# The projection behind a scan: stored expert terms by plain loads, sums on GpSimd, weights turned in the scan's first rounds, roots of two sequences at once

## The chip, the cores and the metric

The kernel runs on one core of a Trainium2 chip. The core has a matmul engine (PE; its weight loads are listed as PEld), a vector engine (DVE), an activation engine (ACT), GpSimd (POOL) and SyncE (SP), which here only issues transfers. Each engine works through its own instructions in order, and the DMA engines work beside them. The metric is the device time of one execution in microseconds (us). All times below are us unless ns is written.

## The reference, cut to what matters

The input `x` is 8 sequences of 1,024 tokens with 256 channels, in 32-bit floats. Two layers follow one another, each of them x plus a sequence mixer plus a mixture of experts, both taken from the same layernorm:

```python
xn = layernorm(x)
# mixer of layer 0: per channel d a state of 16 numbers
h = einsum('dnm,bdm->bdn', A, h) + Bm * x_t
y_t = einsum('dn,bdn->bd', Cm, h) + Dm * x_t
y = gelu(layernorm(y, ln_w, ln_b)) @ W_out.T + b_out
x = x + (xn + y) + experts0(xn)      # 8 experts, 2 of them per token, and a shared one
xn = layernorm(x)
# mixer of layer 1: the softmax runs over an axis of length 1, so every weight is 1
values = sum of (xn @ w_v.T) over the sequence
x = x + values @ w_o.T + experts1(xn)   # 8 experts of 2,048 places, 2 per token
```

The first layer's experts have 128 hidden channels, the second's 1,024. In the second layer a token's gate is its two largest softmax scores divided by their sum.

## The kernel before, in words

Tokens lie on 128 partitions, a tile is 128 tokens: a sequence has 8 tiles (`TPB`), all of them 64 (`NT`). The whole `y`, 64 tiles of 256 channels, stays on the chip. The kernel has five stages.

*Layernorm and first routing (up to about 185).* The normalised `xn` goes into an SBUF tile with rows of `XW` = 264 numbers, of which 256 are used. The shared expert and x are written to an array in DRAM, `base`.

*Finds (about 185 to 288).* The routing has given each pair of a token and an expert a place among 71 blocks (142 columns `NCOL`) of 128 rows. `find` (L694 to L719, 32 calls: 2 choices times 16 groups of 4 tiles) makes one-hot tables on DVE: `hl` says which row (L702), the plane `hh[:, :, 0]` which column (L705); the plane `hh[:, :, 1]` is that times the pair's number plus one, taken from a table `tags` (L709); then plane 0 is multiplied by the token's number in its tile (L712). Four matmuls (L716) sum both into `acc`, and `found` (L721) reads the lists from it.

*Scan (about 288 to 893).* The 256 channels are handled in 8 batches of 32. A batch makes its filters by doubling (`krylov`, levels 1 to 64: matmul L309, copies L316 on DVE and L317 on ACT), carries states from tile to tile (`chunk`: matmul L383, addition L390) and computes outputs (matmul L363, L414) with `xn` as the stationary operand. The blocks of the experts (`block`) are woven in: gather `xb`, matmuls L258 and L269, result `yo` (L767), which an indirect write puts into the DRAM array `yr` (L770), two rows for a token, one for each choice. The loop at the end of the scan deals out finds, blocks, krylov levels and batch steps in one order; finds come during the first batch.

*Projection (893 to 1166).* First `W_out`, `w_o` and the value rows of `w_qkv` are loaded on ACT's queue, turned by PE (L862) and multiplied (L881). Then for every sequence b:

- `start(b)`: a load of `base` into `hb` on SP's queue (L933), two transfers on POOL's queue that add the two rows of `yr` to it (L938), and the moments of `y` (L164, L165, root L166, reciprocal L167);
- `turn(b)`: `off` (L180), 8 normalises on ACT (L182), and matmuls with a flip matrix that turn the tiles, with the gelu (L908) on the way out of PSUM;
- `project(b)`: matmuls with `woutT` (L956), and `y` = PSUM + `hb` on DVE (L963);
- `finish(b)`: moments of the new `y`, `xs` = normalised (L182), its write to `xd`, transposes (L898, copied L904 with sums over tokens), the router's matmuls (L918) and the copy to `logit` (L978);
- `attend(b)`: the token sums spread by POOL (L985), a matmul (L988), `at` (L992), a plain write of `y` to the output (L994) and a transfer on POOL's queue that adds `at` to it (L995);
- `route`, after every second sequence for 16 tiles and after sequences 6 and 7 for 8 tiles each: maximum, exponential (L1007), sum, reciprocal, product, the two best experts, ranks, tables (`hl` L1060, `hh` L1065, L1069, ACT L1073, PE L1075). The first call also runs `no_expert` (L1081).

The order is `start(b+1)`, `project(b)`, `turn(b+1)`, `finish(b)`, `route`, `attend(b)` (L1106 to L1120). A scheduler places the instructions of each engine; the waits between engines follow from the tiles and their buffers.

*Second layer's experts (1166 to 2132).* Gather (L1197), two matmuls (L1213, L1239), and an indirect addition to the output (L1251).

Of the kernel before, what the change touches and what calls it, by code (L numbers as in the profile page):

```python
# [18 lines left out]
P = 128  # L19
# [5 lines left out]
def kernel(  # L25
# [131 lines left out]
    def moments(pool, src, n, mv=None, rstd=None):  # L157

        st = pool.tile([P, n, 6], F32, name="st")
        if mv is None:  # L160
            mv = pool.tile([P, n, 2], F32, name="mv")
            rstd = pool.tile([P, n], F32, name="rstd")
        for i in range(n):
            nc.vector.bn_stats(st[:, i, :], src[:, i, :])  # L164
            nc.vector.bn_aggr(mv[:, i, :], st[:, i, :])  # L165
        nc.scalar.activation(rstd, mv[:, :, 1], AF.Sqrt, bias=epst)  # L166
        nc.vector.reciprocal(rstd, rstd)  # L167
        return mv, rstd

    def normalize(dst, src, mv, rstd, n):  # L170
        for i in range(n):
            nc.vector.tensor_scalar(
                dst[:, i, :], src[:, i, :], mv[:, i, 0:1], rstd[:, i : i + 1],
                ALU.subtract, ALU.mult,
            )

    def normalize_act(dst, src, mv, rstd, n, pool):

        off = pool.tile([P, n], F32, name="off")
        nc.vector.scalar_tensor_tensor(off, mv[:, :, 0], -1.0, rstd, ALU.mult, ALU.mult)  # L180
        for i in range(n):
            nc.scalar.activation(  # L182
                dst[:, i, :], src[:, i, :], AF.Identity,
                bias=off[:, i : i + 1], scale=rstd[:, i : i + 1],
            )
# [23 lines left out]
    with tc.tile_pool(name="xpool", bufs=1) as xpool, tc.tile_pool(name="mo", bufs=2) as mo, tc.tile_pool(  # L209
# [8 lines left out]
        xn = xpool.tile([P, NT, XW], F32, name="xn")  # L218
# [13 lines left out]

        tags = xpool.tile([P, 2, NT], BF16, name="tags")
        nc.gpsimd.iota(tags, pattern=[[1, 2], [2, NT]], base=1, channel_multiplier=0,
                       allow_small_or_imprecise_dtypes=True)

# [43 lines left out]
        def krylov(bt):  # L280
# [23 lines left out]
            def level(k):  # L304
                for g in groups:
                    t = m[g]
                    pk = ps_k.tile([P, 2, 2 * P], F32, name="pk")
                    for j in range(2):
                        nc.tensor.matmul(  # L309
                            pk[:, j, : P + k],  # L310
                            lhsT=t[:, 1 - j, P:],
                            rhs=t[:, j, P - k :],
                            start=True,
                            stop=True,
                        )
                    nc.vector.tensor_copy(t[:, :, P - 2 * k : P - k], pk[:, :, :k])  # L316
                    nc.scalar.copy(t[:, :, P:], pk[:, :, k : k + P])  # L317
# [3 lines left out]
        def rest(bt, toep):  # L321
# [4 lines left out]
            def responses():  # L326
# [26 lines left out]
                nc.vector.memset(made["h"][:, :, :, 0], 0.0)  # L353
# [21 lines left out]
            def chunk(c):  # L375
# [5 lines left out]
                ph = ps_m.tile([P, 512], F32, name="pm")  # L381
                for j, g in enumerate(groups):
                    nc.tensor.matmul(  # L383
                        ph[:, j * NB : (j + 1) * NB],
                        lhsT=m[g][:, 1, P:],
                        rhs=h_t[:, j, :, c],
                        start=True,
                        stop=True,
                    )
                nc.vector.tensor_tensor(  # L390
                    h_t[:, :, :, c + 1],
                    ph[:, : GB * NB].rearrange("p (g b) -> p g b", g=GB),
                    s_t[:, :, :, c],
                    ALU.add,
# [294 lines left out]
        with tc.tile_pool(name="eb", bufs=3) as eb_, tc.tile_pool(name="toep", bufs=2) as toep:  # L689
# [4 lines left out]
            def find(k, i):  # L694
# [11 lines left out]
                    hh[:, :, 0, :], bc(names, 1, [P, 4, NCOL]),  # L706
                    bc(high0[:, k, four], 2, [P, 4, NCOL]), ALU.is_equal,
                )
                nc.vector.tensor_tensor(  # L709
                    hh[:, :, 1, :], hh[:, :, 0, :], bc(tags[:, k, four], 2, [P, 4, NCOL]), ALU.mult  # L710
                )
                nc.vector.tensor_scalar(  # L712
                    hh[:, :, 0, :], hh[:, :, 0, :], tokid[:, 0:1], None, ALU.mult
                )
# [63 lines left out]


# [4 lines left out]
            ] + [found]  # L784
            for bt in range(NBT):
# [9 lines left out]
                for s, step in enumerate(steps):  # L795
                    step()
                    if s % 2 == 0 and s // 2 < len(ahead):
                        ahead[s // 2]()
                    for f in part(s):
# [3 lines left out]
    with tc.tile_pool(name="wmoe", bufs=1) as wmoe, tc.tile_pool(name="tr", bufs=2) as tr, tc.tile_pool(  # L803
        name="xr", bufs=3
    ) as xr, tc.tile_pool(name="rt", bufs=2) as rt, tc.tile_pool(
        name="r1", bufs=1
    ) as r1, tc.tile_pool(name="hot", bufs=2) as hotp, tc.tile_pool(
        name="ps_t", bufs=3, space=PSUM
    ) as ps_t, tc.tile_pool(name="ps_d", bufs=2, space=PSUM) as ps_d, tc.tile_pool(
        name="ps_c", bufs=1, space=PSUM  # L810
    ) as ps_c, tc.tile_pool(name="ps_i", bufs=1, space=PSUM) as ps_i:
# [4 lines left out]
        vals = r1.tile([P, 2, NT], F32, name="vals")  # L816


        QALL = NTOK // P
        place = r1.tile([P, P], BF16, name="place")  # L820
        nc.gpsimd.iota(place, pattern=[[1, P]], base=0, channel_multiplier=0,
                       allow_small_or_imprecise_dtypes=True)
        column = r1.tile([P, 2, E, QPE], F32, name="column")
        for j in range(2):
            nc.gpsimd.iota(column[:, j], pattern=[[QALL, E], [1, QPE]], base=j * (QALL - QPE),
                           channel_multiplier=0, allow_small_or_imprecise_dtypes=True)
        column = column.rearrange("p k e q -> p k (e q)")
        offset = r1.tile([P, 2, E], F32, name="offset")
        nc.gpsimd.iota(offset[:, 0, :], pattern=[[NTOK, E]], base=0, channel_multiplier=0,
                       allow_small_or_imprecise_dtypes=True)  # L830
        nc.gpsimd.iota(offset[:, 1, :], pattern=[[-NTOK, E]], base=1 - NTOK, channel_multiplier=0,
                       allow_small_or_imprecise_dtypes=True)
        sign = r1.tile([P, 2, 2 * TPB], F32, name="sign")
        nc.gpsimd.memset(sign[:, 0, :], 1.0)
        nc.gpsimd.memset(sign[:, 1, :], -1.0)
        go_on = {}
        for n in (TPB, 2 * TPB):
            go_on[n] = r1.tile([P, 2, E, n + 1], F32, name=f"go_on{n}")
            nc.gpsimd.memset(go_on[n], 1.0)
            nc.gpsimd.memset(go_on[n][:, :, :, 0], 0.0)  # L840
        logit = r1.tile([P, 2 * TPB, E], F32, name="logit")
        rowno = r1.tile([P, 2, QPE], F32, name="rowno")
        nc.gpsimd.iota(rowno[:, 0, :], pattern=[[P, QPE]], base=0, channel_multiplier=1,
                       allow_small_or_imprecise_dtypes=True)
        nc.gpsimd.iota(rowno[:, 1, :], pattern=[[-P, QPE]], base=CAP - 1, channel_multiplier=-1,
                       allow_small_or_imprecise_dtypes=True)
        few = r1.tile([P, E], F32, name="few")
        pi = [ps_i.tile([P, 2, P], F32, name=f"pi{j}") for j in range(2)]
        lnw_c = wmoe.tile([P, DC], F32, name="lnw_c")
        nc.scalar.dma_start(lnw_c, ln_w.rearrange("(c p) -> p c", p=P))  # L850
        lnb_c = wmoe.tile([P, DC], F32, name="lnb_c")
        nc.scalar.dma_start(lnb_c, ln_b.rearrange("(c p) -> p c", p=P))

# [440 lines left out]
```

## Time and profile before

| what | us |
| --- | --- |
| three runs, median (lowest to highest) | 2141.95 (2139.48 to 2146.34) |
| the profiled execution | 2139.14 |
| its span in the trace | 2137.4 |
| mean granted PE clock | 0.929 |
| last indirect write of `yr` lands | 895.1 |
| first `xs` normalise (sequence 0) | 939.24 |
| last one (sequence 7) | 1129.41 |
| first matmul of the second layer's experts | 1177.03 |

The times in the trace count from the start of the span. 1.74 us of the profiled execution lie outside the span. Busy time says how long an engine worked in a stretch; the chain of waits says what each instruction that came late had waited for. In a row of groups, the columns are line, engine, operation, output and inputs with their sizes, how many, then busy time, mean ns of one, and the engine's idle time before them with what ended it.

### The profile page before, as it was taken

How to read it: one execution, taken by the hardware profiler on the slowest of the kernel's cores; microseconds unless marked ns; L12 is line 12 of the kernel's file. 1: busy time of each engine (PE TensorE's matmuls, PEld its weight loads, DVE VectorE, ACT ScalarE, POOL GpSimd, SP SyncE). 2: the span in 40 equal slices, each digit the busy share in tenths (PEclk: the TensorE clock that was granted, in tenths of full speed). 3: DMA queues.
4: the chain of work that ended last, by engine and by line, in shares of the span. 5: the costliest groups of instructions: out<-in, count | busy, mean ns of one | idle time of the engine just before them, and what ended most of it. 6: DMA issues, size and time to landing. Idle time of an engine off the chain costs nothing.

```text
span 2137.4 us, 24028 instructions
## 1 busy us (share of the span) xinstructions
PE 1896.7 (89%) x8619; PEld 1409.7 (66%) x8619; DVE 710.9 (33%) x2125; ACT 662.0 (31%) x1450; POOL 811.2 (38%) x818
## 2 busy tenths in 40 slices
PE   6997879888888989577884899999999999999997
PEld 6885558767767776466773466666666666666665
DVE  5878964333334434336665010001010001010000
ACT  4641103222222221167773222222222222222221
POOL 0000021545555556421111644445445455444422
PEclk9998769899999999788886899999999999999999
DMA  9999033444454545599977223232322232232211
GB/s 301 208 197 159 0 99 87 139 140 133 125 154 130 157 136 158 160 218 235 204 157 174 59 38 75 38 79 37 74 38 55 58 60 55 35 77 35 38 20 20
DMA packets 233542, 233.15 MB, mean 109 GB/s; under 512 B 54536, under 2 KB 208976, under 8 KB 233296
## 3 DMA queue, kind: packets, MB, share of 16 engines
q0 software_dynamic: 75584, 104.98, 26.1%
q1 hardware_dynamic: 155152, 124.25, 21.3%
q10 hardware_dynamic: 2688, 2.40, 0.4%
q8 instruction: 68, 1.11, 0.2%
q14 instruction: 50, 0.41, 0.1%
HBM read 136.87 MB, written 97.85 MB: 110 GB/s over the span
## 4 chain that ended last, share of the span: by engine, by line
PE 46%; DVE 4%; ACT 3%; DMA 2%; issue 2%; POOL 0%; ACTq 0%; POOLq 0%; DVEq 0%; SPq 0%
PE phe L1213 21%; PE poe L1239 20%; PE pd L956 2%; PE pd L918 1%; DMA hb<-yr 1%; ACT xs L182 1%; DVE xTe L1208 1%; PE pt L900 1%; DVE st L164 1%; DMA out_dram<-yo,invi 1%; PE pi L1075 1%; PE pc L988 0%; PE pt L898 0%; DVE y L963 0%; DMA hb<-base 0%
## 5 line engine op out<-in xcount | busy, mean ns | idle before, releaser
L1213 PE MATMUL phe<-xTe,w1t 128*128 128x512 f32 x1024 | 450.7, 598 | 16.3 <-DVE xTe L1208 16.3
L1239 PE MATMUL poe<-w2t,hT 128*128 128x256 f32 x2048 | 450.5, 380 | 6.9 <-issue 6.6
L1239 PEld LDWEIGHTS poe<-w2t,hT 128*128 128x128 f32 x2048 | 389.9, 190 | 75.8 <-issue 24.4
L1251 POOL DMA_INDIRECT out_dram<-yo,invi x128 | 204.1, 1595 | 429.9 <-ACT yo L1250 234.5
L1213 PEld LDWEIGHTS phe<-xTe,w1t 128*128 128x128 f32 x1024 | 192.8, 191 | 255.5 <-issue 221.5
L1220 ACT ACTIVATE hT<-phe,b1T 128x512 f32<-128x512 f32 x256 | 175.9, 687 | 306.5 <-PE phe L1213 242.1
L1246 DVE TENSOR_TENSOR yo<-poe,b2t 128x512 f32<-128x512 f32 x64 | 44.3, 692 | 515.5 <-PE poe L1239 487.2
L1250 ACT ACTIVATE yo<-yo,gr 128x256 f32<-128x256 f32 x128 | 58.0, 500 | 422.3 <-DVE yo L1246 422.3
L309 PE MATMUL pk<-kr 128*128 128x129 f32 (+6 forms) x896 | 154.9, 312 | 18.2 <-ACT kr L317 16.8
L309 PEld LDWEIGHTS pk<-kr 128*128 128x128 f32 x896 | 138.4, 207 | 49.1 <-ACT kr L317 22.9
L770 POOL DMA_INDIRECT yr<-yo,goes x142 | 143.1, 1007 | 63.5 <-DVE yo L767 35.0
L258 PE MATMUL pgu<-xT,wb 128*128 128x256 f32 x568 | 148.4, 405 | 14.3 <-ACT xT L247 9.0
L756 POOL DMA_INDIRECT xb<-xnd,choice x142 | 142.1, 1001 | 45.8 <-issue 37.5
L1197 POOL DMA_INDIRECT xg<-xd,invi x128 | 124.3, 971 | 49.2 <-issue 32.0
L317 ACT COPY kr<-pk 128x256 f32<-128x256 f32 x224 | 81.1, 374 | 194.5 <-DVE kr L316 157.6
L1225 POOL DMA_INDIRECT gr<-gd,invi x128 | 124.0, 969 | 45.2 <-issue 36.3
L258 PEld LDWEIGHTS pgu<-xT,wb 128*128 128x128 f32 x568 | 113.6, 206 | 33.8 <-ACT xT L247 10.3
L751 POOL COPY wb<-wrow 1x1 int32<-1x1 int32 x71 | 14.4, 203 | 303.4 <-issue 195.1
L1231 DVE TENSOR_TENSOR gr<-gr,taken 128x4 f32<-128x4 f32 x32 | 5.3, 167 | 343.7 <-DMA gr<-gd,invi 343.7
L269 PE MATMUL pd<-wb,hh 128*128 128x256 f32 x284 | 83.2, 420 | 21.9 <-DVE hh L266 21.3
L263 ACT ACTIVATE sg<-pgu 128x256 f32<-128x256 f32 x87 | 33.4, 384 | 202.8 <-PE pgu L258 149.7
L269 PEld LDWEIGHTS pd<-wb,hh 128*128 128x128 f32 x284 | 55.0, 209 | 46.0 <-DVE hh L266 26.9
(304 smaller groups left out, 2504.1 us busy)
## 6 DMA issues: line engine op xcount, KB each, us to landing
wb<-wpk SPq DMA_DIRECT2D x71, 384.0 KB
xnd<-xn SPq DMA_DIRECT2D x8, 2048.0 KB
hk<-kscr SPq DMA_DIRECT2D x32, 512.0 KB
hb<-yr POOLq DMA_DIRECT2D x16, 1024.0 KB
y<-in_L_attn_x_dram SPq DMA_DIRECT2D x8, 1024.0 KB
base<-bout_t SPq DMA_DIRECT2D x8, 1024.0 KB
base<-y POOLq DMA_DIRECT2D x8, 1024.0 KB
hb<-base SPq DMA_DIRECT2D x8, 1024.0 KB
```

Of the source, the lines that this page charges most:

```text
L258: nc.tensor.matmul(pgu[:, j, :], lhsT=ww[:, c, :], rhs=xT[:, c, :], start=(c == 0), stop=(c == DC - 1),)
L269: nc.tensor.matmul(pd[:, q, :], lhsT=hh[:, q * P : (q + 1) * P], rhs=down, start=True, stop=True)
L309: nc.tensor.matmul(pk[:, j, : P + k], lhsT=t[:, 1 - j, P:], rhs=t[:, j, P - k :], start=True, stop=True,)
L317: nc.scalar.copy(t[:, :, P:], pk[:, :, k : k + P])
L756: nc.gpsimd.indirect_dma_start(out=xb[:, q, : D + 1], out_offset=None, in_=xnd[:, :], in_offset=bass.IndirectOffsetOnAxis(ap=choice[:, 2 * ...
L770: nc.gpsimd.indirect_dma_start(out=next(yr_own)[:, :], out_offset=bass.IndirectOffsetOnAxis(ap=goes[:, 2 * n + q : 2 * n + q + 1], axis=0) ...
L1197: nc.gpsimd.indirect_dma_start(out=xg[:, q, :], out_offset=None, in_=xd[:, :], in_offset=bass.IndirectOffsetOnAxis(ap=invi[:, q0 + q : q0 ...
L1213: nc.tensor.matmul(ph, lhsT=w1t[:, c, h * P : (h + 1) * P], rhs=xT[:, c], start=(c == 0), stop=(c == DC - 1),)
L1220: nc.scalar.activation(hT[:, h], ph, AF.Relu, bias=b1T[:, e * HC + h : e * HC + h + 1])
L1225: nc.gpsimd.indirect_dma_start(out=gr[:, q, :], out_offset=None, in_=gd[:, :], in_offset=bass.IndirectOffsetOnAxis(ap=invi[:, q0 + q : q0 ...
L1239: nc.tensor.matmul(po[:, r, :], lhsT=hT[:, h, q + r, :], rhs=w2t[:, h, :], start=(h == 0), stop=(h == HC - 1),)
L1251: nc.gpsimd.indirect_dma_start(out=of[:, :], out_offset=bass.IndirectOffsetOnAxis(ap=invi[:, q0 + r : q0 + r + 1], axis=0), in_=yo[:, r, : ...
```

## The change

It touches the scan's small parts and most of the projection.

1. `xn`'s rows are 256 numbers long, not 264.
2. `find`: the table `tags` and its multiply on DVE are gone; four multiplies by constants on ACT make plane 1.
3. `krylov`, last level: the first of a group's two matmuls and the ACT copy leave out what nothing reads.
4. `chunk`: each matmul takes the whole state tile of a group (64 columns) and the addition picks the column; the whole tile is set to zero before, not one column in eight.
5. The turning of the weights moves into the list of finds (before the 5th and the 9th call); it borrows the buffers of `wb` and `yo` and loads on ACT's queue. `lnw_c`, `lnb_c` and `wg_t` are loaded on ACT's queue at the kernel's start.
6. `first_moments`, at the last step of the last batch: moments of sequences 0 and 1, one root for both, and the normalise of sequence 0.
7. `load(b)` takes the place of `start(b)`: `base` and the two rows of `yr` by plain loads on SP's queue, added on POOL (for sequence 0 on DVE). `attend` adds `at` to `y` on POOL and writes the output once.
8. One root serves the new `y` of sequence b and the scan's `y` of sequence b + 2 (`measure_two`, `scales`).
9. `route` keeps the exponentials as they are, without sum, reciprocal and product. Sequences 6 and 7 are both routed after the last `finish`, which goes in halves. A small exponential (`ready`) is written before them.
10. The first two experts' `w1` are loaded during sequences 4 and 5. Pools are rearranged: `hb`, `xs` and `yk` have 2 buffers each (`hb` and `xs` had 3), `xT` one (2 before).

```diff
-        xn = xpool.tile([P, NT, XW], F32, name="xn")
+        xn = xpool.tile([P, NT, D], F32, name="xn")
...
                     for j in range(2):
+                        n = k if last and j == 0 else P + k
                         nc.tensor.matmul(
-                            pk[:, j, : P + k],
+                            pk[:, j, :n],
                             lhsT=t[:, 1 - j, P:],
-                            rhs=t[:, j, P - k :],
+                            rhs=t[:, j, P - k : P - k + n],
...
+                    if last:
+                        nc.scalar.copy(t[:, 1, P:], pk[:, 1, k : k + P])
+                    else:
+                        nc.scalar.copy(t[:, :, P:], pk[:, :, k : k + P])
...
-                nc.vector.memset(made["h"][:, :, :, 0], 0.0)
+                nc.vector.memset(made["h"], 0.0)
...
                 for j, g in enumerate(groups):
                     nc.tensor.matmul(
-                        ph[:, j * NB : (j + 1) * NB],
-                        lhsT=m[g][:, 1, P:],
-                        rhs=h_t[:, j, :, c],
-                        start=True,
-                        stop=True,
+                        ph[:, j], lhsT=m[g][:, 1, P:], rhs=h_t[:, j], start=True, stop=True
                     )
...
-                nc.vector.tensor_tensor(
-                    hh[:, :, 1, :], hh[:, :, 0, :], bc(tags[:, k, four], 2, [P, 4, NCOL]), ALU.mult
-                )
                 nc.vector.tensor_scalar(
-                    hh[:, :, 0, :], hh[:, :, 0, :], tokid[:, 0:1], None, ALU.mult
+                    hh[:, :, 0, :], hh[:, :, 1, :], tokid[:, 0:1], None, ALU.mult
                 )
+                for t in range(4):
+                    nc.scalar.mul(hh[:, t, 1, :], hh[:, t, 1, :], float(1 + 2 * (i + t) + k))
...
+            def turn_weights(src, dst):
+                wt = wide("wb")
+                nc.scalar.dma_start(wt, src.rearrange("(r p) d -> p r d", p=P))
+                pm = ps_m.tile([P, 512], F32, name="pm")
+                for c in range(DC):
+                    for r in range(DC):
+                        nc.tensor.transpose(
+                            pm[:, (c * DC + r) * P : (c * DC + r + 1) * P],
+                            wt[:, r, c * P : (c + 1) * P], ident,
+                        )
+                nc.scalar.copy(dst.rearrange("p c d -> p (c d)"), pm)
...
+            def first_moments():
+                for b in range(2):
+                    moments(mo, first_mv[:, b], y[:, b * TPB : (b + 1) * TPB, :], TPB)
+                scales(first_mv, first_rstd, first_off)
+                ys = y[:, :TPB, :]
+                normalize_act(ys, ys, first_rstd[:, 0], first_off[:, 0], TPB)
...
+            finds[4:4] = [lambda: turn_weights(W_out, woutT)]
+            finds[9:9] = [value_weights]
...
+                    if bt == NBT - 1 and s == len(steps) - 1:
+                        first_moments()
...
-            for j in range(2):
-                nc.gpsimd.dma_start(hb, both[j], accum_op=ALU.add)
-            hold[b] = hb, moments(rt, y[:, b * TPB : (b + 1) * TPB, :], TPB)
+            for t in range(0, TPB, 4):
+                some = slice(t, t + 4)
+                yk = xr.tile([P, 4, 2, D], F32, name="yk")
+                nc.sync.dma_start(yk, both[:, some])
+                for j in range(2):
+                    (nc.gpsimd if b else nc.vector).tensor_tensor(
+                        hb[:, some, :], hb[:, some, :], yk[:, :, j, :], ALU.add
+                    )
+            hold[b] = hb
...
+        def measure_two(b):
+            n = 2 if b + 2 < NB else 1
+            mv = rt.tile([P, n, TPB, 2], F32, name="mv")
+            if n == 2:
+                moments(rt, mv[:, 1], y[:, (b + 2) * TPB : (b + 3) * TPB, :], TPB)
...
-            mine = of[b * S : (b + 1) * S, :].rearrange("(i p) d -> p i d", p=P)
-            nc.sync.dma_start(mine, y[:, b * TPB : (b + 1) * TPB, :])
-            nc.gpsimd.dma_start(mine, bc(at, 1, [P, TPB, D]), accum_op=ALU.add)
+            ys = y[:, b * TPB : (b + 1) * TPB, :]
+            nc.gpsimd.tensor_tensor(ys, ys, bc(at, 1, [P, TPB, D]), ALU.add)
+            nc.sync.dma_start(of[b * S : (b + 1) * S, :].rearrange("(i p) d -> p i d", p=P), ys)
...
-            sm = rt.tile([P, n], F32, name="sm")
-            nc.vector.tensor_reduce(sm, pr, AX.X, ALU.add)
-            nc.vector.reciprocal(sm, sm)
-            nc.vector.tensor_tensor(pr, pr, bc(sm, 2, full), ALU.mult)
...
-        start(0)
+        load(0)
         turn(0)
+        early = []
         for b in range(NB):
             if b + 1 < NB:
-                start(b + 1)
+                load(b + 1)
+            measure_two(b)
             project(b)
             if b + 1 < NB:
                 turn(b + 1)
-            finish(b)
-            if b % 2 == 1 and b < NB - 1:
+            finish(b, TPB if b < NB - 1 else TPB // 2)
+            if b == NB - 1:
+                ready = rt.tile([P, 1], F32, name="ready")
+                nc.scalar.activation(ready, epst, AF.Exp)
+                for j in range(2):
+                    ends = route((b - 1 + j) * TPB, TPB, ends)
+            elif b % 2 == 1:
                 ends = route((b - 1) * TPB, 2 * TPB, ends)
-            if b >= NB - 2:
-                ends = route(b * TPB, TPB, ends)
+            if NB - 4 <= b < NB - 2:
+                early.append(first_weights(b - NB + 4))
             attend(b)
```

## The prediction

> **What bounds the kernel now.** I read the page's first two parts, then the busy time by stage, then the chain of waits, then groups of instructions. The slices show four stretches.
>
> ```profile
> span 2137.4 us, 24028 instructions
> PE 1896.7 (89%) x8619; PEld 1409.7 (66%) x8619; DVE 710.9 (33%) x2125; ACT 662.0 (31%) x1450; POOL 811.2 (38%) x818
> PE   6997879888888989577884899999999999999997
> DVE  5878964333334434336665010001010001010000
> ```
>
> A digit is 53.4 us. DVE has 8 and 9 in slices 3 and 4, where the pair tables are made ("finds"); PE has 8 and 9 through the scan; slices 16 to 21 (855 to 1175 us) hold the end of the scan and the projection, with PE down to 5; from there PE is full. The second-layer experts, 964 us, are untouched. The finds by stretches of 20 us (columns: length, then PE, PE loads, DVE, ACT and POOL busy, granted PE clock, DMA share, GB/s):
>
> ```profile
> 200.00:220.00 20.00, 14.14 (x60) 11.15 (x61) 17.82 (x42) 2.14 (x6) 0.00 (x0) 0.50 0.05 3
> 220.00:240.00 20.00, 16.23 (x121) 14.11 (x121) 19.41 (x49) 5.21 (x14) 0.00 (x0) 1.00 0.00 1
> 240.00:260.00 20.00, 15.82 (x47) 6.55 (x46) 18.35 (x33) 1.81 (x6) 0.00 (x0) 0.77 0.00 0
> 260.00:280.00 20.00, 17.15 (x80) 14.04 (x79) 19.26 (x40) 0.00 (x0) 0.00 (x0) 0.50 0.00 1
> ...
> L709 DVE TENSOR_TENSOR wb<-wb,tags 128x568 bf16<-128x568 bf16 x32 | 23.8, 744 | 0.0
> L716 PE MATMUL pgu<-wb,xb 128*128 128x284 bf16 x128 | 30.7, 385 | 15.3 <-DVE wb L712 15.3
> ```
>
> DVE is full (17.8 to 19.4 of 20), PE close behind at a granted clock of 0.50 to 1.00, ACT nearly idle. The two rows below the stretches are groups: the multiply by `tags`, and the matmul that waits for DVE. The projection opens with a chain of transfers (start, length, what):
>
> ```profile
> 892.66 2.42 DMA yr<-yo,goes
> ...
> 895.42 6.81 DMA hb<-base
> ...
> 902.77 13.71 DMA hb<-yr
> ...
> 916.77 10.29 DMA hb<-yr
> ...
> 927.19 0.70 DVE y L963
> ```
>
> The last scatter lands at 895.1; the first sum on `y` waits until 927.2 for a load and two accumulating transfers. The first `xs` normalise starts at 939.24; those of the other sequences at 963.89, 985.98, 1027.92, 1052.03, 1080.66, 1103.69 and 1129.41. Over 939.24 to 1166.00 PE is busy 177.8 of 226.8 us, DVE 146.0, ACT 155.3, POOL 32.0: an alternating chain with slack on each engine.
>
> **The change part by part**, in us of the profiled execution (2139.14, of which 1.74 lie outside the span; the median of three, 2141.95, is 2.8 above).
>
> *Finds.* L709 goes: 32 x 0.744 = 23.8 of DVE, whose work of one find is 0.685 + 0.744 + 0.744 + 0.365 = 2.54. Added are 128 ACT multiplies; the like at L1073 takes 0.297, so 38 of ACT unpipelined, under ACT's idle time (9.2 busy of the 100 from 200 to 300). Then PE is next: 70.3 busy in the same 100, so at a share of 0.9 the stretch is 78. Bounds: 4 (PE at half clock keeps the pace) and 21 (DVE's time goes whole); PE's 14 to 17 of 20 lies between, so **-12**.
>
> *Krylov.* The last level's first matmul has 64 columns for 192: 128 of 384 columns of a group. The 128x192 row is 0.329 x 96 = 18.5 for 24 groups between 300 and 880, so a third is 0.26 a group, 8 for 32 groups; the rows of 128x132 (0.283) and 128x192 (0.329) of that stretch differ by far less than their columns, which says 0 to 4. Bounds 0 and -8, **-4**. ACT's copy of half the size is off the path.
>
> *Scan states.* L383 now takes a group's 64 contiguous columns, not 8 strided ones. Group rows: 0.251 for 8 columns, 0.306 for 64 at L414. 384 instructions give up to +21 unhidden, but 288 of them between 300 and 880 were priced at half clock or better in both rows, and a chunk of 8 took 0.95 at 220.55 (0.12 each), like L918's 64 columns: **0** (-3 to +5). The full memset (128x256) is some 0.2 x 8 of DVE, hidden under PE there. The narrower `xn` row is read by L363 and L414; no row says that its 1,024-byte stride is slower, and DVE's strided writes at L424 are not: 0, a rival below.
>
> *Weights.* Their turning (PE 1.28 + 1.28 + 3.78 at L862 and L881) leaves the projection's opening, where the transfers cover it, so nothing is gained there; it enters the finds, where PE has the next bound: +4 at most. Its DMAs stand in ACT's queue, behind which the krylov copies stand, and wait for a `wb` slot. Three small ACT loads go ahead at the kernel's start. **+2** (0 to +5).
>
> *Opening.* The accumulates go. After the scatter, put 2 later (895.1 to 897) because 16 moment pairs (0.40 + 0.17, some 9 of DVE), a square-root table load (1.28) and 8 normalises (4.04) now sit among the last blocks, SP brings base and two halves of the terms, 3.1 MB. At 230 to 300 GB/s (the windows' 224 to 235 and the page's 301) that is 10.5 to 13.7: 909. The last adds on DVE are two of 128x1024: 2 x 0.68 (a 128x512 add at L662) each 1.36, so 2.7; four sums of 0.68 follow, then moments 0.6, load and root 1.6, small ones 0.6: `xs` at 918 to 922 against 939.2. Before, b=1's normalise (4.04) and its gelus stood in between too. **-19** (-10 to -24). b=1 then needs its 3.1 MB and four POOL adds: 897 + 6.2 MB at 250 GB/s = 922, +5 to +10 gives 927 to 932; its project comes some 12 after 920, at 932. It just fits.
>
> *Eight sequences.* POOL gets four adds of 128x1024 and one of 128x2048 each, and loses about 2 x 1.55 + 1.55 of descriptor writing. No row has a POOL add. Lower bound: the copy of 128x256, one input, alone takes 0.40, so 1.6 and 3.2. Upper: two inputs at that price each, 3.2 and 6.4. Per sequence 4 x 1.6 + 3.2 + 0.4 = 10.0 to 19.6. I take the middle, 14.8 of a mean period of 28.3: POOL fits. SP's order is hazardous (a write of `out` waits for POOL's add and stands ahead of the `hb` load two sequences on), but that load has two periods: about 14 of slack by 28.3 x 2 less 12 project-to-attend, 4.8 add, 7 load, 9.6 adds and waits.
>
> Does POOL's reading slow DVE? This row and its neighbours speak for it (the times of L751's copies are 175 shortest, 178 median and 1819 ns longest):
>
> ```profile
> 288.02 1.94 POOL L751 COPY wb<-wrow 1x1 int32<-1x1 int32 x2 [106.70 <-DVE xb L702]
> 288.19 0.74 DVE L705 TENSOR_TENSOR wb<-names,high 128x568 bf16<-128x568 bf16 x1
> 288.85 0.28 DVE L329 TENSOR_TENSOR cm<-maskg,c_in 128x128 f32<-128x128 f32 x1
> 289.05 0.74 DVE L709 TENSOR_TENSOR wb<-wb,tags 128x568 bf16<-128x568 bf16 x1
> ```
>
> One POOL copy of a single word stood until 289.96, just past three two-input DVE instructions that end at 289.79. So one of them waits; that DVE waits for POOL likewise is not shown. Priced so: `off` at L180, on the path once a sequence, meets POOL at 14.8/28.3 = 0.52 for half an add (1.5): 0.8 x 8 = 6. Three routes run beside POOL's adds; 2 each on the path: 6. **+12**; lower end 0 (no blocking), upper 37: if DVE (18.25 a sequence) and POOL (14.8) exclude each other, the period is 33.0 against 28.3, x 8.
>
> [...]
>
> *Routes and tail.* Five routes drop three DVE instructions (0.25 + 0.22 + 0.25), half on the path: **-1.5**. Roots of two sequences at once spare no table load as they are ordered: 24 loads now (11 + 8 + 5), about as many after, since gelus and roots still alternate; 0. At the end route 6 joins route 7 after the last finish; its 16 ACT multiplies (3.3) come before route 7's exponential, and the write of `out` waits for a POOL add of 3 to 6 before the gathers. The halved finish gains some 2. **+2** (-3 to +8).
>
> Sum: -12 - 4 + 0 + 2 - 19 + 12 - 1.5 + 2 = -20.5, so 2118.6 for a profiled execution and **2121** on the median's scale.
>
> **The rivals.**
> A. *POOL and DVE exclude each other, and POOL is dearer.* For: the 1.6 lost at 288. Against: the stage's longest DVE group, the moments (96 x 0.402 = 38), reads one input. The rest of the sum is -32.5, so it decides from +32.5, or 4.1 a sequence; at the middle of 37 (POOL 14.8) and 76 (POOL 19.6: 18.25 + 19.6 - 28.3 = 9.5, x 8), +56: 2142 + 24 = **2166**, slower.
> B. *Finds don't shorten.* PE at clock 0.50 keeps the pace and turning the weights is unhidden: -4 and +4 in place of -12 and +2: **2131**. For: PE 17.15 of 20 at clock 0.50. Against: 15.3 of PE's wait is put down to L712.
> C. *No blocking.* The +12 falls away: **2109**. For: POOL's copies at L985 took 0.52 and 0.56 beside DVE's L1069 at 1111.94 and 1138.29, against 0.40 alone: they overlapped.
> D. *The narrower rows are slower to read.* L414 is busy for 76.0 and L363 for 65.4: 20% of that is +28, so **2149**. Nothing in the trace points to it, and it decides from 15% on.
>
> **How the numbers follow.** Forecast 0.44, A 0.20, B 0.15, C 0.15, D 0.06. A measurement can tell 0.3% (6.4) from no change. Faster (under 2135.5): the forecast 0.42, B 0.11, C 0.15, A 0.01, D 0.01, together 0.70; same 0.08 (forecast 0.02, B 0.03, A 0.02, D 0.01); slower 0.22 (A 0.17, D 0.04, B 0.01). The range runs from 2090 (C with finds at -20 and the opening at -24) to 2163 (A's middle); the forecast's own is 2106 to 2134.
>
> **What would show it.** L709 gone, DVE no longer full at 200 to 280, finds over 12 sooner; first `xs` at about 906 (939.2 - 12 - 4 + 2 - 19); first-layer rows L363 and L414 unchanged per instruction; POOL adds of 2 to 3 us; DVE's two-input rows (`off`, the tables at L1060 and L1065) at their old lengths of 0.155 and 1.22. Wrong if these lengthen by the POOL adds' length, if PE waits for a POOL add of `hb`, or if the second-layer experts start later after the last `xs` than 47.6 (1129.41 to 1177.03).

## The result, and the profile after

The changed kernel takes 2177.75 us (median of 4 runs, 2172.11 to 2181.89), the kernel before 2143.16 beside it: a ratio of 1.016 (95% interval 1.0131 to 1.0189). Run twice more later it came out at 1.0115 (1.0081 to 1.0149) and 1.0091 (1.0064 to 1.0117). It is slower, by some 20 to 35 us; a gain had been forecast, 2121, with a range up to 2163.

The page of the changed kernel, its span and the slices that answer to those of before (40 equal slices, counted from 0, of 54.5 us each):

```profile
span 2180.2 us, 24131 instructions
...
PE   6998889989888888777776699999999999999996
...
DVE  5877843434343443556756101011000010110100
...
PEclk9998989989998998767776799999999999999998
```

The granted clock before, for comparison:

```profile
PEclk9998769899999999788886899999999999999999
```

DVE is down from 9 to 8 in slice 4, in the finds, but slices 17 to 22, the projection, are worse: PE is no busier than 7, and the granted clock is 6 or 7; before, the projection's slices 17 to 21 had 8 but for the last of them. Cut at the same events, the two profiled executions differ so (us from event to event; the finds end with their last matmul, the `yr` write counts from its start):

| stretch | before | after | difference | forecast |
| --- | --- | --- | --- | --- |
| start to the end of the finds | 291.4 | 278.6 | -12.7 | -12, and 2 for the weights |
| to the last `yr` write | 601.3 | 611.4 | +10.1 | -4, and some 2 for the moments |
| to the first `xs` | 46.5 | 25.4 | -21.1 | -19, less those 2 |
| eight sequences, to the second layer's first matmul | 237.8 | 298.2 | **+60.4** | +12.5 |
| second layer | 960.4 | 966.6 | +6.2 | 0 |

The two executions are 42.8 apart, where -20.5 had been forecast. Of the 63 between, some 48 lie in the sequences, 12 in the scan and 6 in the second layer. From `xs` to `xs` the sequences took 24.7, 22.1, 41.8, 24.2, 28.6, 23.0, 25.7 and 47.6 to the end; now 28.9, 28.8, 56.8, 31.4, 40.1, 30.8, 28.7 and 52.8. The third, fifth, and the last two hold routes; even the others are 4 to 8 longer. Here are the first two by stretch (length, busy time of PE, PE loads, DVE, ACT and POOL, clock, DMA share, GB/s), before:

```profile
939.24:963.89 24.65, 20.79 (x116) 17.86 (x116) 9.69 (x42) 17.07 (x35) 5.50 (x5) 0.86 1.00 224
963.89:985.98 22.09, 16.18 (x81) 13.22 (x81) 11.13 (x49) 13.82 (x30) 1.96 (x2) 0.81 1.18 235
```

and after:

```profile
915.42:944.31 28.89, 25.06 (x116) 21.37 (x116) 10.32 (x43) 16.96 (x33) 18.75 (x8) 0.72 0.73 240
944.31:973.12 28.81, 23.55 (x84) 18.61 (x84) 11.91 (x50) 14.21 (x32) 9.72 (x5) 0.64 0.69 244
```

PE runs the same 116 matmul records in the first one (the trace has two records for each f32 matmul here) and takes 4.3 more for them; DVE and ACT do what they did. PE's clock fell from 0.86 to 0.72. In the second-layer router's matmuls it can be read directly (records of L918 before and L976 after: shortest, median and longest in ns):

```profile
L918 PE MATMUL pd<-wg_t,xT x256: 219/275/421, 944.8 to 1140.5; 128*128 128x64 f32 x128
```

```profile
L976 PE MATMUL pd<-wg_t,xT x256: 219/421/476, 921.0 to 1174.2; 128*128 128x64 f32 x128
```

By the trace's list of clock changes, 15 of the 256 started at half clock before, and 164 after. Where the routes run, DVE shows something else (timeline of the changed kernel: start, length, instruction):

```profile
1058.77 9.36 POOL L901 TENSOR_TENSOR hb<-hb,yk 128x1024 f32<-128x1024 f32 x4 [18.07 <-DVE st L175]
...
1059.35 1.86 DVE L182 SCALAR_TENSOR_TENSOR off<-mv,rstd 128x16 f32<-128x16 f32 x1
...
1061.23 2.31 DVE L1050 TENSOR_TENSOR posi<-pos,sign 128x32 int32<-128x32 f32 x1
...
1063.80 2.04 DVE L1052 TENSOR_SCALAR cut<-posi 128x32 int32<-128x32 int32 x1
...
1065.93 2.23 DVE L1055 CAST cutb<-cut 128x32 bf16<-128x32 int32 x1
...
1068.09 4.51 POOL L1000 TENSOR_TENSOR y<-y,at 128x2048 f32<-128x2048 f32 x1
1068.16 4.47 DVE L1028 COPY tot<-cum 128x16 f32<-128x16 f32 x1
```

Each of these small DVE instructions takes 0.15 to 0.19 elsewhere. Here it lasts until the POOL addition that runs beside it is over: one after each of the four additions of 2.34, and 4.47 beside the one of 4.51. They stand in the chain of waits. Two theories follow from this:

- **Theory 1**: POOL's additions hold DVE's instructions up. Summed, DVE's overlong instructions in the eight sequences exceed their usual length by about 34 (24 in nine executions of lines that run several times, and some 10 in four lines that run once, in `no_expert`).
- **Theory 2**: PE's granted clock stays at half longer after the wait for `xs`: 17.1 where it was 6.8, by the list of clock changes, in the sequences without a route.

The rival to both was that the other moved parts (moments of two sequences, both last routes at the end, DVE's own load) make the sequences long.

### The profile page after: what moved, and what is told of

Same layout as the page of the kernel before. It is cut to its first block, busy times and chain, and to the rows that moved or that the text cites. A ratio compares the mean times of both kernels' runs of the same rounds, so it can differ in the third digit from the quotient of the medians.

```text
span 2180.2 us, 24131 instructions
## 1 busy us (share of the span) xinstructions
PE 1925.5 (88%) x8619; PEld 1436.7 (66%) x8619; DVE 730.0 (33%) x2070; ACT 687.5 (32%) x1568; POOL 871.8 (40%) x829
## 4 chain that ended last, share of the span: by engine, by line
PE 47%; DVE 6%; ACT 2%; issue 2%; DMA 1%; another core or an unknown queue 1%; POOL 0%; POOLq 0%; ACTq 0%; DVEq 0%
PE phe L1255 21%; PE poe L1281 20%; PE pd L932 2%; PE pd L976 2%; DVE xTe L1250 1%; PE pt L878 1%; ACT xs L187 1%; DVE st L175 1%; PE pt L962 1%; DMA out_dram<-yo,invi 1%; PE pi L1078 0%; ACT hh L1076 0%; DVE hl L1063 0%; DVE hh L1068 0%
## 5 line engine op out<-in xcount | busy, mean ns | idle before, releaser
L1255 PE MATMUL phe<-xTe,w1t 128*128 128x512 f32 x1024 | 450.4, 598 | 16.4 <-DVE xTe L1250 16.4
L312 PEld LDWEIGHTS pk<-kr 128*128 128x128 f32 x896 | 137.1, 208 | 42.0 <-issue 21.1
L312 PE MATMUL pk<-kr 128*128 128x129 f32 (+7 forms) x896 | 154.0, 309 | 11.0 <-ACT kr L323 9.3
L323 ACT COPY kr<-pk 128x256 f32<-128x256 f32 x192 | 69.1, 374 | 127.0 <-DVE kr L319 103.3
```

Source lines behind the costliest of these rows:

```text
L312: nc.tensor.matmul(pk[:, j, :n], lhsT=t[:, 1 - j, P:], rhs=t[:, j, P - k : P - k + n], start=True, stop=True,)
L1255: nc.tensor.matmul(ph, lhsT=w1t[:, c, h * P : (h + 1) * P], rhs=xT[:, c], start=(c == 0), stop=(c == DC - 1),)
```

## The experiments

The chips were of two kinds: on some the kernel before took 2141 to 2146, on others 2051. The scan made most of the difference: one kernel was profiled on both kinds (that of experiment 7), and from the end of the finds to the last `yr` write it took 585.6 on the former and 507.3 on the latter, in its second layer 959.8 and 950.2, while its periods in the sequences agreed to 0.1. Each ratio is against the kernel before on the same chip; where that was a 2051 chip, it says so. The changed kernel itself ran on chips of the first kind alone, so what experiments 1 to 3 gain over it is read from the time of the eight sequences, 298.2 in its profile. "Periods" are those from `xs` to `xs` and the last one to the second layer.

**1. All additions on DVE** (`adds_on_dve`).

```diff
-                    (nc.gpsimd if b else nc.vector).tensor_tensor(
+                    nc.vector.tensor_tensor(
...
-            nc.gpsimd.tensor_tensor(ys, ys, bc(at, 1, [P, TPB, D]), ALU.add)
+            nc.vector.tensor_tensor(ys, ys, bc(at, 1, [P, TPB, D]), ALU.add)
```

> The changed kernel with all adds of hb and of at on DVE, so that POOL reads nothing but the small vb. Theory 1 (POOL's adds hold DVE's instructions up): the DVE instructions of 2.2 to 5.5 us among the routes (together 34 us above their usual length, nearly all on the chain) go back to 0.2 to 1.2, and the periods with routes shrink; DVE gets 32 x 1.22 + 8 x 2.4 of work, part of it on the path: about 2155 for 2178. Theory 2 (the loss is PE's clock, which stays at half for 17 us after each wait for xs in place of 6.8): less DVE waiting changes little where no route runs; periods without a route stay 28 to 31, total 2165 or more. If both were wrong, nothing changes (2178) or it is slower for DVE's load.

2041.02, ratio 0.9947 (0.9929 to 0.9966) on a 2051 chip. Periods 29.2, 28.5, 47.0, 30.4, 33.8, 30.6, 23.3, 49.7, together 272.5. Those with routes fall by 9.7, 6.3 and 5.4 and the end by 3.2, those without stay, with 16 to 21 of half clock in each. No DVE instruction is held up any more: L1050, L1052 and L1055 take 0.19 at most. DVE's additions cost 1.22 each for `hb` and 2.29 for `at`. Theory 1 holds for the routes, and theory 2's part is untouched, as it said.

**2. Two wide matmuls ahead of the router's** (`wide_matmuls_before_logits`), and **3. PE kept busy while ACT makes `xs`** (`pe_kept_busy`). Both do extra work whose result nothing uses.

```diff
+            for i in range(2):
+                nc.tensor.matmul(pr[:, 0, :], lhsT=xT[:, 0, :P], rhs=woutT[:, 0, :], start=True, stop=True)
```

```diff
                 turn(b + 1)
+                busy(6)    # six matmuls of 512 columns into a tile of ps_t
```

> The changed kernel with two extra matmuls of 256 columns between the transposes and the router's 64-column matmuls in each sequence; their result is overwritten. They stand where the kernel before had two of the projection's matmuls. Theory 2 (the granted clock returns to full sooner when wide matmuls follow the transposes; the 64-column ones keep it at half): the half-clock stretch after the xs of sequences without a route falls from 17.1 to about 7, the router's matmuls go from 0.213 to 0.112 each, the periods without a route fall from 28.9 to about 25: some 15 to 25 us in all, about 2158. Theory 1 or a rival by which the clock's length has another cause: 8 x 1.7 us of extra work, about 2190.

> The changed kernel with six extra matmuls of 512 columns (about 1.05 us each) after the flips of the next sequence, so that PE has no gap while ACT makes xs; their result is read by nothing. Theory 2: no half clock in the periods without a route, these fall from 28.9 to about 23 to 25, total about 2145 or less. Theory 1: the extra 6.3 us of PE work a sequence take the place of an idle 4 to 7, no gain: 2178 to 2195.

Ratios 1.0022 (0.9998 to 1.0047) and 1.0009 (0.9998 to 1.0021) on a 2051 chip. With the wide matmuls the half clock falls to 7.0, 6.8 and 6.8 in the first, fourth and sixth periods, and the four without a route to 26.0, 24.5, 27.2 and 26.3, 1.7 of which is the extra work itself. With PE kept busy it is 0 in the fourth and the sixth (25.2 and 25.3), though 15.8 in the first; the third period, with a route, grows to 62.2, and in its trace the extra matmuls stand among the route's. The eight sequences take 278.0 and 285.8. Theory 2 holds, and how long the half clock lasted here depended on what PE did after the gap, not only on the gap.

**4. Both remedies** (`dve_adds_and_wide`), with the changed kernel and the kernel before once more.

> Both remedies at once: adds on DVE and two wide matmuls before the logits. If theories 1 and 2 are two separate losses, they add: periods without a route about 26, 24.5, 27, 26 as with the wide matmuls alone, those with a route 43, 30 and 23: some 15 below the adds on DVE alone, so 2025. If DVE's load takes the place of POOL's, no better than 2041.

> The changed kernel once more, beside the kernels it is compared with. The first four runs showed the kernel before at 2051, with the scan's eight batches 77 apart in place of 95. Theories 1 and 2 both say that the loss sits in the eight sequences, which should be the same to 1 us as in the first profile (periods 28.9, 28.8, 56.8, 31.3, 40.1, 30.8, 28.7 and 52.8 to the second layer). If the scan's parts are worth -33 here, as measured alone, and the opening -19, with +60 for the sequences, the sum is 2051 + 8 = 2059; if the loss between 630 and 847 in the first profile belongs to the change, it is about 2072.

> The kernel before once more, for a profile on the same chip. If the 92 between its first and its later times come from one place, it is the scan (77 a batch for 95), with less half clock there; the sequences keep their periods of 24.7, 22.1, 41.8, 24.2, 28.7, 23.0, 25.7.

0.9986 (0.9962 to 1.001); periods 26.3, 24.4, 46.1, 31.1, 33.2, 26.0, 26.1, 51.1, together 264.4. The remedies add in part: 34 below 298.2, where 26 and 20 alone would make 46. The fourth period misses: it has 17.4 of half clock although its two wide matmuls stand ahead of the router's, so they do not always suffice. The fifth, with a route, has 16.4. The ratio is no better than that of the additions on DVE alone (0.9947), but that one is from the other kind of chip. The changed kernel again: 1.0115, on chips of the first kind; its periods repeat to 0.1 (in its third run, below, to 2.3). The kernel before, once more on a chip of the first kind, has its old periods to 0.2.

**5. The two loops around the transposes** (`loops_as_before`, and the reverse in the kernel before, `before_with_new_loops`). Which edit had put the router's matmuls at half clock could be read from the order of PE's instructions. `finish` nests the loops over token halves (`hf`) and channel halves (`c`) the other way round than before; the list of the change above does not have this. The scheduler then puts 9 router matmuls, one of the projection and 7 router matmuls after the transposes; before it was 1, then 2 of the projection's 256 columns, then 15.

```diff
-                for hf in range(t // 4, (t + n) // 4):
-                    for c in range(DC):
+                for c in range(DC):
+                    for hf in range(t // 4, (t + n) // 4):
```

> The changed kernel with the two loops around the transposes of xs in the old nesting (channel halves outside, token halves inside); nothing else. The scheduler then puts one router matmul, two projection matmuls and 15 router matmuls on PE after the transposes, as in the kernel before, in place of 9, 1 and 7. Theory 2 in its sharper form (the loop order alone makes the half clock last 17 us): half clock 7 to 9 in the periods without a route, these 24.5, 23, 25, 24 in place of 28.9, 28.8, 31.3, 30.8; POOL's adds and the routes' stalls stay. Some 20 to 25 below the changed kernel, ratio to the kernel before about 1.002 where the changed kernel has 1.0115. If the extra matmuls helped for another reason, 1.01.

> The kernel before with only those two loops swapped as in the change. Sharper theory 2: half clock 16 to 17 in place of 6.8 after each xs, four periods without a route 4 to 5 longer and those with a route 2 to 4: +20 to +28, ratio 1.010 to 1.013. If the order matters only together with POOL's adds: 1.000.

With the old nesting the changed kernel has 0.9995 (0.9973 to 1.0017), its loss gone, and periods 24.8, 21.5, 58.3, 24.7, 41.1, 25.5, 28.5, 51.5: without routes as before the change, with routes as long as ever. The kernel before with the new nesting has 1.0137 (1.0098 to 1.0177), and 29.1, 26.0, 43.9, 28.5, 28.0, 29.5, 26.1, 52.7, with 13.7 or 17.1 of half clock after `xs` in those without a route. PE's timeline in one sequence (start, length, what, and the count of records), changed kernel first, then the same with the old nesting:

```profile
944.96 5.13 PE L962 MATMUL pt<-ident,xs 128*128 128x128 f32 x16 [3.68 <-ACT xs L187]
949.89 3.94 PE L976 MATMUL pd<-wg_t,xT 128*128 128x64 f32 x18
953.62 1.17 PE L932 MATMUL pd<-woutT,gT 128*128 128x256 f32 x2
954.58 3.09 PE L976 MATMUL pd<-wg_t,xT 128*128 128x64 f32 x14
957.46 8.74 PE L932 MATMUL pd<-woutT,gT 128*128 128x256 f32 x28
```

```profile
918.25 5.07 PE L962 MATMUL pt<-ident,xs 128*128 128x128 f32 x16 [3.69 <-ACT xs L187]
923.16 0.33 PE L976 MATMUL pd<-wg_t,xT 128*128 128x64 f32 x2
923.33 1.08 PE L932 MATMUL pd<-woutT,gT 128*128 128x256 f32 x4
924.24 3.46 PE L976 MATMUL pd<-wg_t,xT 128*128 128x64 f32 x30
927.54 6.26 PE L932 MATMUL pd<-woutT,gT 128*128 128x256 f32 x28
```

The gap before the transposes is 3.68 and 3.69. In the first, 18 records take 3.94 (0.22 each, half clock) and the next 14 likewise, and the projection starts at half; in the second, after four wide records, 30 take 3.46 (0.115) and the projection 6.26 for 8.74. The stretches say the same, for the old nesting in the changed kernel:

```profile
892.81:917.59 24.78, 20.51 (x116) 17.48 (x116) 10.29 (x43) 16.63 (x33) 18.70 (x8) 0.84 0.77 252
```

and for the new nesting in the kernel before, where POOL adds nothing:

```profile
944.50:973.60 29.10, 25.40 (x116) 21.62 (x116) 9.67 (x42) 17.12 (x34) 5.60 (x5) 0.71 1.02 199
```

**6. Old nesting and additions on DVE** (`old_loops_and_dve_adds`), and **accumulating transfers for all but sequence 0, with the old nesting** (`accumulate_except_first`; `at` too is added by a transfer, as before).

```diff
+            if b >= 1:
+                for j in range(2):
+                    nc.gpsimd.dma_start(hb, both[j], accum_op=ALU.add)
```

> The changed kernel with the old loop nesting and all adds on DVE. If POOL's hold on DVE is what is left of the loss, the sequences take about what they took before plus what the adds cost DVE on the routes' path (58.3 to 45, 41.0 to 32, the rest 24 to 25, 22, 25, 25, 23 to 25): 10 to 20 below the old loops alone, ratio 0.990 to 0.995 where that had 0.9995. If the routes are long for another reason (moments of two sequences on DVE, ps_c shared), no gain: 0.999.

> The changed kernel with the old loop nesting, and with plain loads and adds only for sequence 0 (on DVE); for the others hb is summed by accumulating transfers, and at is added by one, as before. Theories 1 and 2 say that the sequences then take what they took before (periods 24.7, 22.1, 41.8, 24.2, 28.7, 23.0, 25.7, tail 48), while finds (-13) and the opening (-15 to -20; b = 1 may be late, as its accumulates start after sequence 0's loads) stay: ratio 0.984 to 0.988. If the sequences stay long for another reason (moments of two sequences at once, both routes at the end), 0.995 or more.

0.9865 (0.9833 to 0.9896), with 25.1, 21.7, 49.3, 25.6, 30.3, 24.9, 24.2, 48.3; and 0.9901 (0.9866 to 0.9936), with 31.3, 23.0, 46.6, 24.6, 36.1, 26.2, 23.0, 46.8. The first settles the split: eight sequences of 298.2 in the changed kernel, 275.9 with the old nesting, 272.5 with DVE's additions, 249.4 with both. So the nesting is worth 22 to 23, and POOL's additions in place of DVE's some 26, whichever is taken first. Some 11.6 remain over the 237.8 of before, 7.5 of it in the third period. DVE's own additions are among them; how much of the 11.6 they or the other moved parts make was not separated. The second kernel has no additions on DVE after sequence 0 and does not bring the old time back either: 257.7, with the third period at 46.6 for 41.8, the fifth at 36.1 for 28.6, and a first one of 31.3, late as its expectation had allowed.

**7. The scan's parts alone** (`scan_parts_alone` on a 2051 chip, `scan_parts_again` beside `changed_third` on one of 2144), and with the turning of the weights (`scan_and_weights`). Each is the kernel before with those parts of the change and nothing else.

> The kernel before with only the scan's parts of the change: narrower xn rows, find without the DVE multiply, the shorter last krylov level, the 64-column state matmuls. Prediction's terms: -12 - 4 + 0, so 2126. If the 13 us that the changed kernel loses again between the scan's sixth batch and its end (630 to 847 us) come from these parts (the clock at half there for 41 us in place of 24), the gain is 3 to 8 only: 2135 to 2140.

> The scan's parts alone once more. On a chip of the slower scan (before at 2140 to 2146): if its gain is -12 to -16 there (ratio 0.9925 to 0.9945), the changed kernel's scan (-12) is just these parts, and the -33 belongs to the faster chip; if it is -33 there too (0.985), something else in the change costs the scan 20.

> The changed kernel a third time, to have it on the same chip as the scan's parts: ratio 1.01 to 1.016 on a chip with the kernel before at 2143; on one with 2051, 1.004 to 1.01, since the sequences' loss is the same and the scan's gain is larger.

> The kernel before with the scan's parts and the weights turned among the finds. If the turning costs the scan what the changed kernel lost there (the last yr at 877 to 890 in place of 861), the last yr comes some 15 to 20 later and the ratio is 0.988 to 0.992 on a chip with the kernel before at 2143; if it is hidden, 0.982 as without it, or a little less, as the opening loses its wait for the weights.

0.9847 (0.9822 to 0.9872) and 0.9823 (0.9792 to 0.9853): -33 and -37, twice the 16 forecast, on either kind of chip; with the weights 0.9812 (0.979 to 0.9834), on a 2051 chip, so the turning costs nothing that shows there. On 2051 chips the scan after the finds took 507.3 with these parts alone, 509.7 with the weights, and 509 to 511 in the three kernels with the rest of the change too: 2 to 3 more, where 4 had been forecast for weights and moments. On the others it took 601 to 603 in three profiles with the scan of before, 585.6 in the one profile of these parts, and 590 to 612 in ten profiles of kernels that have the changed kernel's scan. So there the gain outside the finds, some 16 with these parts alone, is on average not seen with the whole change. That the rest of the change costs the scan something on those chips is possible; why, and how much beside such a spread, stays open.

**8. The projection of the next sequence ahead of the transposes**, so that PE has 7 us of wide matmuls to do while ACT makes `xs`: `project_first` (additions on DVE, new nesting), `old_loops_dve_project_first`, `accumulate_and_project_first` (experiment 6's second kernel in this order, old nesting) and `scan_and_project_first` (the kernel before with the scan's parts).

```diff
-            project(b)
+            if b == 0:
+                project(0)
             if b + 1 < NB:
                 turn(b + 1)
+                project(b + 1)
             finish(b, TPB if b < NB - 1 else TPB // 2)
```

> Adds on DVE, and the projection of sequence b + 1 ahead of the transposes and logits of sequence b, so that PE has 7 us of wide matmuls to do while ACT makes xs. Theory 2: PE's gap before the transposes goes, the clock stays full there, and the period without a route falls to about 22 (PE's own work 20.8): about 2010. If the sum on y then waits for hb (DVE adds, late loads) the gap only moves: 2040.

> The same with the projection of sequence b + 1 first. The loop nesting should matter little here, as wide matmuls fill PE's gap anyway: 0.984 to 0.989, as the kernel of that order with the new nesting (0.9885). If it is 0.98 or less it beats the accumulating one (0.983).

> The same with the projection of sequence b + 1 ahead of the transposes of sequence b. Periods without a route fall to 16 to 23 as in the earlier kernel of that order, and DVE has no adds of hb: those with a route fall to 42 and 29 from 48.5 and 35: ratio 0.972 to 0.980. If the accumulates (1 MB at 10 to 14 us, two in a row) are too slow for the shorter period, y waits for hb and it is no better than 0.986.

> The kernel before with the scan's parts and the projection of sequence b + 1 ahead of the transposes of sequence b. Theory 2: PE's gap is filled, periods without a route fall from 24.7, 22, 24.2, 23 to 16 to 21: 12 to 20 below the scan's parts alone, ratio 0.973 to 0.977. If the accumulating transfers can't keep up (as in the first periods of the accumulating kernel of that order, 29 and 25), 0.980 to 0.983.

Ratios 0.9885 (0.9848 to 0.9921), 0.9817 (0.9776 to 0.9858), 0.9833 (0.9798 to 0.9868) and, on a 2051 chip, 0.9829 (0.9807 to 0.985). Single periods fall to 16 and 19, with no half clock in some, but the first accumulating one grows (29.2 and 31.8), as `hb` is wanted sooner. The second, 2104.18, is the fastest with the change's projection and beats both kernels; it is no better than the scan's parts with the old projection (2106.79 on the same chip), which miss the opening's 21. In the fourth the new order gains nothing over the scan's parts alone (0.9847), where 12 to 20 us had been expected.

## Why the prediction was wrong

In the sequences +12.5 had been forecast and +60.4 was measured: 22 from the swapped loops, which the sum did not have, some 26 from POOL's additions where it had 12, and 11.6 not separated. Point by point, by its own steps:

- *Finds* (-12, and +2 for the weights): right; -12.7 to their end, so rival B is out. From 200 to 280 DVE has 16.0 to 18.0 of each 20 us, and ACT 8.0 to 12.4.
- *Krylov, scan states, narrower rows* (-4, 0, 0): not settled. The scan's parts alone gave 33 to 37; in the profile on a chip of the first kind the finds end 16 sooner and the scan after them is 16 shorter, for the 4 forecast. How these divide was not tried. In the changed kernel the scan came out 10 longer, and 3 longer and 3 shorter in its repeats, beside the 601.3 of before; this stays open. The rival of slower narrow rows (D) is out: the 128x512 matmuls on `xn` had a median of 1036 ns after (L369) against 1098 before (L363), the 128x64 ones 288 (L415) against 298 (L414).
- *Opening* (-19): right; -21.1 from the last write of `yr` to the first `xs`, and -21 by its own count from there (920 less 897, for 939.2 less 895.1). The first `xs` came at 915.4 and not at about 906, because of the scan.
- *POOL's prices* (middle of 1.6 and 3.2, and of 3.2 and 6.4): right; the medians are 2.36 (L901) and 4.54 (L1000).
- *POOL against DVE* (+12): the mechanism was right and the term too small; the runs put it at some 26 over the same additions on DVE. So rival C, no blocking, is out. It went wrong in two places. The pricing of the routes took 2 a route, while in one sequence alone L182, L1050, L1052, L1055 and L1028, as shown above, stand for 12.5 of the chain of waits, because these dependent small instructions waited, one after the other, for POOL additions of 2.34 and 4.51. And the argument went by DVE instructions with two inputs: the TENSOR_SCALAR, the CAST and the COPY above read one tensor each and were held as well, for 2.04, 2.23 and 4.47. Rival A, which had DVE and POOL exclude each other, foresaw the sign with a price of 56; it measured half that, less than the 32.5 from which it would have decided alone.
- *PE's time per sequence*: the step that failed. The prediction took the profile's "alternating chain with slack on each engine" to keep its speed, named PE's clock for the finds and the scan but not for the sequences, and priced the new `finish` without its swapped loops, which put them at nothing. That order alone cost the kernel before 1.4% (26 in its sequences), and the changed kernel 22 to 23. No rival held it.
- *Routes and tail* (-1.5 and +2): the end is 5.2 longer, of which additions on DVE take 3.2 back. The second layer's 6.2, which the forecast had at nothing, was not tried; the old nesting alone had 962.2 there for 966.6, and on 2051 chips kernels with and without the change's projection were 1 to 2 apart (951 to 952 against 950).
- *The signs*: `off` reached 1.86 once, a table at L1068 5.54 once, and the second layer started 52.8 after the last `xs`; these spoke against the forecast as it had said they would. PE never waited for a POOL addition of `hb`.
- *The range*: its ends do not follow from the terms. Rival A's middle is 2166 on the median's scale, not 2163, and C with the finds at -20 and the opening at -24 is 2096, not 2090. 2178 lies beyond either.

With the old nesting and the additions on DVE the same change comes out at 0.9865, or 28 faster. That this is near the 21 that had been forecast is partly luck: the 21 include 12 for POOL's additions, which this kernel does not have, and its sequences are 11.6 longer than before.

## What to carry to other kernels

Where PE's work has a gap, look at what its next instructions are, and try the wide ones first: the place of two wide matmuls in each sequence decided 22 to 26 us here (experiment 5), and a swapped loop nest in the source moved them. One period of experiment 4, the fourth with its 17.4 of half clock, shows that it does not always help. Before giving GpSimd elementwise work, list the small dependent instructions that the vector engine has at that time; here such instructions of 0.15 to 0.19 lasted 1.86 to 2.31 beside additions of 2.34, and 4.47 beside one of 4.51, those with a single input among them. And compare the order of instructions on each engine, not only the diff.

## What the hardware showed

- Ahead of the transposes in the four sequences without a route PE had gaps of 3.58 to 3.94 in the kernel before, and of 6.55 and then 3.68 to 3.95 in the changed one. By the list of clock changes the granted clock went to half 2.4 to 4.4 us after the last matmul before, for 6.8 each time; in the changed kernel it did so 4.1 to 5.2 after it, for 17.1 each time, although PE had no gap from the transposes on. After the transposes came 2 records of 64 columns and then 4 of 256 in the kernel before, 18 of 64 columns in the changed one. With two wide matmuls put first (experiments 2 and 4) the half clock was 6.8 to 7.0 in three periods of the former and 17.4 in one of the latter. Why the order has this effect no run shows.
- DVE instructions of 0.15 to 0.19 lasted 1.86 to 2.31, or 4.47, beside POOL additions of 2.34 and 4.51; POOL's own additions at L901 stayed within 2.338 to 2.410. The moments (L175, one input) kept their 0.39 to 0.43.
- The scan of one and the same kernel took 585.6 on one chip and 507.3 on another, with 80.4 and 19.2 us of half clock in it, while the projection's periods agreed to 0.1. Why chips differ so was not tried.
